# A two-layer cross-attention kernel: the scores of a visit in two PSUM tiles, all maxima at once, and softmax portions recorded ahead of a product

## The chip, the cores and the metric

The kernel runs on one core of a Trainium2 chip. TensorE (PE) multiplies matrices and writes PSUM, VectorE (DVE) and ScalarE (ACT) read PSUM and work on SBUF, GpSimd (POOL) and SyncE (SP) issue DMAs, and POOL adds a few sums. All data are float32. The metric is the device time of one execution in microseconds (us); several executions give a median.

## The reference

Two cross-attention layers follow each other, for 8 batch elements with 100 query tokens of width 640, in 20 heads of 32. The context has 722 tokens of width 1024: 77 text tokens and 645 "ip" tokens. A layer attends to both parts, with a softmax over each part by itself:

```
q  = x @ Wq;  k, v = text @ Wk, text @ Wv;  k_ip, v_ip = ip @ Wk_ip, ip @ Wv_ip      (split into 20 heads)
layer 0:  a = softmax(q k^T * scale) v + softmax(q k_ip^T * scale) v_ip
layer 1:  sem = scale * (softmax(q_full k_full^T * scale) @ text) @ ip^T             (one for all heads)
          a = softmax(q k^T * scale) v + mask * softmax(q k_ip^T * scale + 0.5 * sem) v_ip
x  = a @ Wo + bias + x
```

## The kernel before

A unit `u` is one batch element in one layer: 0 to 7 are layer 0, 8 to 15 layer 1. Units go in pairs. The main loop makes 80 visits `(u, c)`: a visit is the attention of one unit for one group of four heads (`c` from 0 to 4, four heads of 32 in the 128 partitions).

**The attention of a visit.** `scores(u, c, part)` multiplies q and k of four heads: part 0 gives the first 512 ip columns, part 1 the other 133 ip columns and the 77 text columns. Both parts write one PSUM tile `sc` of four banks, a bank for each head. Of each part DVE takes the negative maximum of each row (in layer 0 L953, one instruction for several heads; in layer 1 L960, one for each head, which also adds `sem` and writes the sum to SBUF), and ACT takes the exponential with that maximum as bias and sums it up (L968, one for each head). Text columns have their own maximum, addition and exponential (L974, L976, L984). Small instructions (L979 to L991) turn the two partial maxima and sums into factors; `scaled` (L997, ACT) and `scaled_rest` (L1001, L1005, DVE) multiply the probabilities. In the visit after, `transposes` has TensorE transpose them in six blocks (`pspt`, L1030), which DVE (L1037) or ACT (L1035) copy to SBUF, and `values` multiplies them with v (`pv`) and copies the result out (L1056).

**Portions.** These steps aren't recorded at once. `scores` records the first maxima and puts the rest as portions (closures) into the list `later`. A portion is taken from it by `emit(1)`, which `next_task` calls after each production task that has time of its own; by `free_scores()` at the start of `scores`, as far as the tile `sc` must be free; and by `transposes(..., 0)`, which takes all that are left.

**Production.** The keys and values of the pairs to come are made in between, by Strassen-Winograd products with seven products in place of eight: `seven()` gives seven tasks (L179 to L226), each with products on TensorE and then a copy from PSUM on ACT (first L193, second L202) or an addition on DVE (sixth L198, seventh L208, fifth L213, fourth L219, third L224). The names are psk for keys, psv for values, and psvk for the `two_chunks` products of the last pair. Sums of tokens and of weights that the products need are DVE work (L134 to L137 for the weights, `weight_sums`; L232, L233 and others for the tokens; and, for `two_chunks`, the `begin` task with two later sums, L725 and L726). `spread` gives every task a due time from estimated costs; `make` and `apart` take the tasks due.

**Small work.** `between` splits each visit into four stretches and puts small steps there: `out_piece` (the output product `pso` of a finished pair, and the addition of bias and residual L863), `q_piece` (the queries of layer 1), and in layer 1 the four steps of `sem` (`sem_text` with the copy `g`, `sem_logits`, `sem_transpose` with the copy `tpt`, `sem_scores` with the copy `sem`). They and `pspt` share one PSUM pool.

**The order of the engines.** Only TensorE's is pinned:

```
    with tc.manual_schedule(engines={mybir.EngineType.PE}):
```

Its instructions run as recorded. For DVE, ACT, POOL and SP the framework's scheduler chooses an order from what is recorded; each engine then runs its queue strictly in that order.

Of the kernel before, what the change touches and what calls it, by code (L numbers as in the profile page):

```python
# [9 lines left out]
F32 = mybir.dt.float32  # L10
AF = mybir.ActivationFunctionType
ALU = mybir.AluOpType
AX = mybir.AxisListType

P = 128
B = 8
S = 100
C = 640
CC = 1024
NT = 77  # L20
NI = 645
# [3 lines left out]
KB = NK - KA  # L25
# [19 lines left out]
def two_layer_xattn(  # L45
# [17 lines left out]
    nc = tc.nc  # L63
# [636 lines left out]
    def last_visits(visits):  # L700

        xs, lists = {}, []
        for i, (j, tasks_of) in enumerate(visits):

            def begin(i=i):
                if i == 0:
                    xs.update(places[LAST])
                elif i + 2 < len(visits):
                    xs[i + 2] = load_x(LAST, visits[i + 2][0])

            lists.append([(0.0, begin)] + tasks_of(j, xs, i))
        return lists

    def two_chunks(r, j, xs, at):
        n0, n1 = BLOCKS[j]
        n = n1 - n0
        sums, o, made, late = {}, {}, {}, []

        def begin():
            t = spool.tile([P, 3, HK, 2, NX], F32, tag="s", name=f"sl_{r}_{j}")  # L720
            a11, a12, a21, a22 = quarters(xs[at], n)
            s1, s2, s4 = (t[:, i, :, 0, :n] for i in range(3))
            sums.update(token_sums(a11, a12, a21, a22, s1, s2, None, s4))
            sums[7] = a21
            late.append(lambda: nc.vector.tensor_tensor(a21, a11, a21, ALU.subtract))  # L725
            late.append(lambda: nc.vector.tensor_tensor(s4, a12, s2, ALU.subtract))  # L726
            o[0] = opool.tile([P, 2, 2, P + NX], F32, tag="made", name=f"vko_{r}_{j}")

        def product(ps, which, go_on):
            for k in range(HK):  # L730
                nc.tensor.matmul(
                    ps[:, :P], lhsT=sums[which][:, k, :P], rhs=W["v", WHICH[which]][:, k, r * P : (r + 1) * P],
                    start=(k == 0 and not go_on), stop=(k == HK - 1), skip_group_check=True,
                )
            for k in range(HK):
                nc.tensor.matmul(
                    ps[:, P : P + n], lhsT=W["k", WHICH[which]][:, k, r * P : (r + 1) * P], rhs=sums[which][:, k, :],
                    start=False, stop=(k == HK - 1), skip_group_check=True,
                )

        def step(i):
            if i == 0:
                made[0] = seven(
                    f"psvk_{r}_{j}", product, tuple(o[0][:, h, m, : P + n] for h in range(2) for m in range(2))
                )
            made[0][i]()
            if i < 6:
                return
            for h, u in enumerate(LAST):
                nc.gpsimd.dma_start(  # L750
                    k_d[u][:, :4, n0:n1].rearrange("p (m r) n -> p r m n", r=2)[:, r], o[0][:, h, :, P : P + n]
                )
                nc.gpsimd.dma_start(
                    v_d[u][j * P : (j + 1) * P, : 4 * P].rearrange("p (m r n) -> p r m n", m=2, r=2)[:, r],
                    o[0][:, h, :, :P],
                )

        steps = [(1.8, lambda i=i: step(i)) for i in range(7)]
        sums_ = [(0.0, lambda i=i: late[i]()) for i in range(2)]
        return [(0.0, begin)] + steps[:1] + sums_[:1] + steps[1:4] + sums_[1:] + steps[4:]  # L760

    def fifth_chunk(kinds, j, xs, at):
        n0, n1 = BLOCKS[j]
        tasks = []
        for kind in kinds:
# [28 lines left out]
                        nc.gpsimd.dma_start(v_d[u][j * P : (j + 1) * P, 4 * P :], t[:, i, :P])  # L794

            tasks += [(1.8, lambda h=h, f=half: f(h)) for h in range(2)]
        return tasks


    sem_state, gs = {}, {}  # L800
# [125 lines left out]
    def emit(n):  # L926
        for _ in range(n):
            later.pop(0)[1]()

    def free_scores():  # L930

        emit(max([i + 1 for i, (r, _) in enumerate(later) if r], default=0))

    def scores(u, c, part):
        k0, k1 = ((0, KA), (KA, NK))[part]
        free_scores()
        if part == 0:
            pr[u, c] = ppool.tile([S, 4, NK], F32, tag="p", name=f"p_{u}_{c}")

            stats[u, c] = stat.tile([S, 14, 4], F32, tag="st", name=f"st_{u}_{c}")  # L940
        sc = ps_sc.tile([P, 4, 512], F32, tag="sc", name=f"sc_{u}_{c}_{part}")
        for i in range(4):
            rows = slice(32 * i, 32 * i + 32)
            nc.tensor.matmul(  # L944
                sc[:S, i, : k1 - k0], lhsT=qs_[u][rows, c, :], rhs=ks[u, c][rows, k0:k1], start=True, stop=True
            )
        p, st, l = pr[u, c], stats[u, c], u // B
        n = min(k1, NI) - k0
        lo, f, rz, mul = st[:, 6, :], st[:, 7:9, :], st[:, 9:11, :], st[:, 11:13, :]

        def maxima(heads):
            if l == 0:
                nc.vector.tensor_reduce(  # L953
                    st[:, part, heads[0] : heads[-1] + 1], sc[:S, heads[0] : heads[-1] + 1, :n], AX.X, ALU.max,
                    negate=True,
                )
                return
            for i in heads:

                nc.vector.tensor_tensor_reduce(  # L960
                    out=p[:, i, k0 : k0 + n], in0=sc[:S, i, :n], in1=sems[u][:, k0 : k0 + n], scale=-1.0,
                    scalar=3.0e38, op0=ALU.add, op1=ALU.min, accum_out=st[:, part, i : i + 1],
                )

        def exponentials(heads):
            for i in heads:
                dst = p[:, i, k0 : k0 + n]
                nc.scalar.activation(  # L968
                    dst, dst if l else sc[:S, i, :n], AF.Exp, bias=st[:, part, i : i + 1],
                    scale=-1.0 if l else 1.0, accum_out=st[:, 3 + part, i : i + 1],  # L970
                )

        def text_maxima():
            nc.vector.tensor_reduce(st[:, 2, :], sc[:S, :, n:KB], AX.X, ALU.max, negate=True)  # L974

            nc.vector.tensor_tensor(  # L976
                p[:, :, NI:], sc[:S, :, n:KB], st[:, 2, :].unsqueeze(2).to_broadcast([S, 4, NT]), ALU.add
            )
            nc.vector.tensor_tensor(lo, st[:, 0, :], st[:, 1, :], ALU.min)  # L979
            nc.vector.tensor_tensor(f, lo.unsqueeze(1).to_broadcast([S, 2, 4]), st[:, 0:2, :], ALU.subtract)  # L980

        def text_exponentials():
            nc.scalar.activation(f, f, AF.Exp)
            nc.scalar.activation(p[:, :, NI:], p[:, :, NI:], AF.Exp)  # L984
            nc.vector.tensor_reduce(st[:, 5, :], p[:, :, NI:], AX.X, ALU.add)
            nc.vector.tensor_tensor(st[:, 3:5, :], st[:, 3:5, :], f, ALU.mult)
            nc.vector.tensor_tensor(st[:, 4, :], st[:, 3, :], st[:, 4, :], ALU.add)

        def factors():
            nc.vector.reciprocal(rz, st[:, 4:6, :])  # L990
            nc.vector.scalar_tensor_tensor(  # L991
                mul, f, mask_sb[:, l : l + 1], rz[:, 0:1, :].to_broadcast([S, 2, 4]), ALU.mult, ALU.mult
            )

        def scaled(heads):
            for i in heads:
                nc.scalar.activation(p[:, i, :KA], p[:, i, :KA], AF.Copy, scale=mul[:, 0, i : i + 1])  # L997

        def scaled_rest(text):
# [4 lines left out]
            else:  # L1004
# [2 lines left out]
                    ALU.mult,  # L1007
                )

        if part == 0:  # L1010
            maxima((0, 1))
            later.append((True, lambda: (exponentials((0, 1)), maxima((2, 3)))))
            later.append((True, lambda: exponentials((2, 3))))
        else:
            maxima((0, 1, 2, 3))
            later.append((True, lambda: (exponentials((0, 1, 2, 3)), text_maxima())))
            later.append((False, text_exponentials))
            later.append((False, lambda: (factors(), scaled((0, 1)), scaled_rest(False))))
            later.append((False, lambda: (scaled((2, 3)), scaled_rest(True))))

    pts = {}

# [38 lines left out]
    def production():  # L1061
# [44 lines left out]
        for kinds, js in (("kv", every[:2]), ("k", every[2:]), ("v", every[2:])):  # L1106
            visits += [(j, lambda j, xs, i, kinds=kinds: fifth_chunk(kinds, j, xs, i)) for j in js]
        lists = last_visits(visits)
        lists[0][1:1] = v_last[2:3]
        lists[0][3:3] = v_last[3:]  # L1110
        for a, b, tasks in (
            (n - 10 - AHEAD, n + 2.9, lists[: 2 * NB]),
            (n + 2.9, n + 6.9, lists[2 * NB : 3 * NB]),
# [97 lines left out]
    with tc.manual_schedule(engines={mybir.EngineType.PE}):  # L1211
# [6 lines left out]
        done = [0]  # L1218

        def next_task():  # L1220
            todo[done[0]][2]()
            if todo[done[0]][0] and later:
                emit(1)
            done[0] += 1

        def make(until):
# [13 lines left out]
        def between(n, a, b, small):  # L1240

            mark[0] = done[0]
            near = 0.4 if n < NC_ * LAST[0] + 6 else 0.1
            for i, (_, f) in enumerate(small):
                make(n + a + (b - a) * (i + 1) / (len(small) + 1))
                apart(n + b + near)
                f()
            make(n + b)
            apart(n + b + near)
# [86 lines left out]
```

## Time and profile before

| | |
|---|---|
| Median of 3 runs (lowest to highest) | 2071.68 us (2071.6 to 2073.09) |
| Profiled execution | 2071.6 us |
| Its span, between first and last instruction | 2069.8 us |
| Mean granted TensorE clock | 0.998 of full speed |
| PE busy | 2043.5 us (99%) |
| PE's weight loads busy (beside its products) | 1581.2 us (76%) |
| DVE busy | 1074.8 us (52%) |
| ACT busy | 799.6 us (39%) |
| POOL busy | 309.9 us (15%) |

A line of the timeline gives start and duration in us, engine, source line, operation, what it writes and from what, and how many instructions are taken together; in brackets stand the engine's idle time before it and the instruction that ended it ("1.51 <-ACT p L968": idle for 1.51 us until ACT's line 968, which wrote p, was done). A duration holds the instruction's own latency, so that the start of the next can lie before its end. A line of the waits names the waiting engine and line, what it waited for, the time in total, how often, and the longest.

### The profile page before, as it was taken

The numbers are of one execution on the slowest core, as the hardware profiler recorded it, in microseconds if no ns is written. First come the engines' busy times: TensorE is split into PE (matmuls) and PEld (weight loads), VectorE is DVE, ScalarE is ACT, GpSimd is POOL, SyncE is SP. The second block draws the span as 40 slices with busy tenths as digits, with TensorE's granted clock in tenths as the row PEclk, the third lists the DMA queues.
The fourth block names the chain that finished last, engine by engine and source line by source line (L and its number), as shares of the span: only waits on it lengthen the run. The fifth ranks groups of instructions, "written<-read, shape, count | busy, mean of one in ns | idle before, by whom it ended". The sixth has DMA issues, their size and how long they took to land.

```text
span 2069.8 us, 38196 instructions
## 1 busy us (share of the span) xinstructions
PE 2043.5 (99%) x15122; PEld 1581.2 (76%) x15122; DVE 1074.8 (52%) x2789; ACT 799.6 (39%) x2271; POOL 309.9 (15%) x445
## 2 busy tenths in 40 slices
PE   9999999999999999999989999999999999999998
PEld 8676767677778777786778777787778778889787
DVE  2211322355554655455475555455555557777676
ACT  1001000244433434344333444435444445565576
POOL 3212312111111111010110111010111111111120
PEclk9999999999999999999999999999999999999999
DMA  9545313232424433262543533262434345545472
GB/s 327 155 132 171 97 56 105 88 107 71 129 83 131 129 113 91 81 179 65 160 133 103 147 105 106 72 178 75 115 89 134 90 133 151 158 133 140 121 211 74
DMA packets 302544, 255.35 MB, mean 123 GB/s; under 512 B 46686, under 2 KB 271378, under 8 KB 302366
## 3 DMA queue, kind: packets, MB, share of 16 engines
q1 hardware_dynamic: 280590, 184.48, 32.2%
q0 software_dynamic: 21776, 68.44, 9.5%
q8 instruction: 119, 1.95, 0.4%
q14 instruction: 59, 0.48, 0.1%
HBM read 183.93 MB, written 68.93 MB: 122 GB/s over the span
## 4 chain that ended last, share of the span: by engine, by line
PE 95%; DVE 2%; DMA 1%; ACT 1%; issue 1%; POOL 0%; SPq 0%; ACTq 0%; DVEq 0%
PE psv_a L597 8%; PE psv_d L597 8%; PE pspt L1030 8%; PE psk_d L625 6%; PE psk_a L625 6%; PE sc L944 6%; PE psk L563 5%; PE psv_e L597 4%; PE pv L1052 4%; PE psv_c L597 4%; PE psv_b L597 4%; PE psk_e L625 3%; PE psk_c L625 3%; PE psk_b L625 3%; PE pso L858 3%; PE psq L275 2%
## 5 line engine op out<-in xcount | busy, mean ns | idle before, releaser
L968 ACT ACTIVATE p<-sc,st 100x512 f32<-100x512 f32 (+1 forms) x320 | 166.4, 528 | 218.5 <-DVE st L953 218.2
L1037 DVE COPY pt<-pspt 128x400 f32<-128x400 f32 x319 | 175.5, 569 | 122.8 <-PE pspt L1030 116.6
L997 ACT ACTIVATE p<-p,st 100x512 f32<-100x512 f32 x320 | 208.5, 713 | 62.8 <-DVE st L991 62.7
L968 ACT ACTIVATE p<-p,st 100x512 f32<-100x512 f32 (+1 forms) x320 | 177.1, 555 | 132.3 <-DVE st L960 131.8
L1030 PEld LDWEIGHTS pspt<-ident,p 100*128 100x128 f32 (+1 forms) x1920 | 188.0, 137 | 42.1 <-issue 5.0
L1030 PE MATMUL pspt<-ident,p 100*128 100x100 f32 (+1 forms) x1920 | 211.0, 250 | 5.7 <-DVE res L863 2.4
L597 PE MATMUL psv_a<-wv,x 128*128 128x397 f32 (+1 forms) x560 | 185.0, 472 | 1.3 <-ACT vo L193 1.3
L646 POOL DMA_DIRECT2D k_d<-ko x140 | 99.5, 715 | 527.6 <-DVE ko L219 470.9
L597 PE MATMUL psv_d<-wv,s 128*128 128x320 f32 (+1 forms) x560 | 174.9, 455 | 0.0
L1035 ACT COPY pt<-pspt 128x400 f32<-128x400 f32 (+1 forms) x161 | 78.4, 487 | 227.7 <-PE pspt L1030 227.3
L953 DVE TENSOR_REDUCE st<-sc 100x2 f32<-100x1024 f32 (+1 forms) x120 | 126.3, 1052 | 59.4 <-ACT p L968 30.5
L597 PEld LDWEIGHTS psv_a<-wv,x 128*128 128x128 f32 x560 | 103.5, 190 | 63.7 <-issue 8.1
L960 DVE CUSTOM_DVE_ANT_0 p<-sc,sem 100x512 f32<-100x512 f32 (+1 forms) x320 | 139.7, 489 | 22.5 <-PE sc L944 22.3
L597 PEld LDWEIGHTS psv_d<-wv,s 128*128 128x128 f32 x560 | 103.4, 190 | 57.4 <-issue 5.5
L625 PE MATMUL psk_a<-x,wk 128*128 128x256 f32 (+1 forms) x672 | 137.2, 350 | 4.2 <-ACT ko L193 4.2
L944 PE MATMUL sc<-k,q 32*100 32x210 f32 (+1 forms) x1280 | 138.6, 502 | 0.8 <-ACT p L968 0.6
L625 PE MATMUL psk_d<-s,wk 128*128 128x256 f32 (+1 forms) x672 | 136.4, 348 | 0.0
L612 POOL DMA_DIRECT2D v_d<-vo x70 | 38.3, 548 | 642.4 <-DVE gst L587 317.5
L563 PE MATMUL psk<-x,wk 128*128 128x256 f32 (+1 forms) x560 | 132.0, 383 | 0.0
L625 PEld LDWEIGHTS psk_a<-x,wk 128*128 128x128 f32 x672 | 110.8, 192 | 24.7 <-issue 6.0
L563 PEld LDWEIGHTS psk<-x,wk 128*128 128x128 f32 x560 | 102.8, 189 | 25.7 <-issue 9.9
L625 PEld LDWEIGHTS psk_d<-s,wk 128*128 128x128 f32 x672 | 108.3, 189 | 17.5 <-issue 5.2
(209 smaller groups left out, 3234.5 us busy)
## 6 DMA issues: line engine op xcount, KB each, us to landing
x<-ip_t SPq DMA_DIRECT2D x84, 512.0 KB
k<-k_d SPq DMA_DIRECT2D x80, 322.5 KB
v<-v_d SPq DMA_DIRECT2D x80, 320.0 KB
v_d<-vo POOLq DMA_DIRECT2D x70, 320.0 KB, 2.5
k_d<-ko POOLq DMA_DIRECT2D x112, 128.0 KB, 4.3
x<-ip_t SPq DMA_DIRECT2D x22, 532.0 KB
o<-wo SPq DMA_DIRECT2D x35, 320.0 KB
q<-wq SPq DMA_DIRECT2D x20, 320.0 KB
```

The source lines that it names most:

```text
L563: nc.tensor.matmul(ps[:, : 2 * n], lhsT=W["k", 4][:, k, :], rhs=x_all[:, at[j], :, k, :n], start=(k == 0), stop=(k == NCC - 1),)
L597: nc.tensor.matmul(ps[:, :m], lhsT=tokens(k)[:, :P], rhs=w[:, k, :], start=(k == 0 and not go_on), stop=(k == HK - 1), skip_group_check=True,)
L625: nc.tensor.matmul(ps[:, i * m : (i + 1) * m], lhsT=W["k", WHICH[which]][:, k, r * P : (r + 1) * P], rhs=tokens(k), start=(i == 0 and k == ...
L646: nc.gpsimd.dma_start(dst[:, :, r], ko[0][:, h, :, i, p0 : p0 + n])
L944: nc.tensor.matmul(sc[:S, i, : k1 - k0], lhsT=qs_[u][rows, c, :], rhs=ks[u, c][rows, k0:k1], start=True, stop=True)
L953: nc.vector.tensor_reduce(st[:, part, heads[0] : heads[-1] + 1], sc[:S, heads[0] : heads[-1] + 1, :n], AX.X, ALU.max, negate=True,)
L960: nc.vector.tensor_tensor_reduce(out=p[:, i, k0 : k0 + n], in0=sc[:S, i, :n], in1=sems[u][:, k0 : k0 + n], scale=-1.0, scalar=3.0e38, op0= ...
L968: nc.scalar.activation(dst, dst if l else sc[:S, i, :n], AF.Exp, bias=st[:, part, i : i + 1], scale=-1.0 if l else 1.0, accum_out=st[:, 3 ...
L997: nc.scalar.activation(p[:, i, :KA], p[:, i, :KA], AF.Copy, scale=mul[:, 0, i : i + 1])
L1030: nc.tensor.transpose(ps[:rows, i * S : (i + 1) * S], pr[u, c][:, i, j * P : j * P + rows], ident[:S, :S])
L1037: nc.vector.tensor_copy(dst, src)
L1052: nc.tensor.matmul(ps[32 * i : 32 * i + 32, :S], lhsT=lhs, rhs=pt[:rows, j, i * S : (i + 1) * S], start=(j == 0), stop=(j == 5),)
```

## The change

1. `scores` writes two tiles `sc0` and `sc1` of two banks (heads 0 and 1, heads 2 and 3) in place of one of four.
2. The maxima of all four heads are recorded at once, by pairs of heads. In layer 0, part 1, these are two instructions in place of one; the text maxima and the text addition also go by halves, and are recorded with them, the differences too. The later portions are shared out anew: `factors` and the 133 columns of `scaled_rest` in one, the scaling by ACT in the two after it.
3. Part 0 first takes all that is left in `later`; part 1 calls `free_scores()` as before.
4. `next_task` takes a portion before the task in place of after it, and `between` takes one before each small step.
5. The token sums of a visit of the last pair's products (`begin` of `two_chunks`) are joined to the last task of the visit before; two parts of the last weight sums move to later places in the first list.

```diff
--- before.py
+++ after.py
@@ -708,7 +708,12 @@
                 elif i + 2 < len(visits):
                     xs[i + 2] = load_x(LAST, visits[i + 2][0])
 
-            lists.append([(0.0, begin)] + tasks_of(j, xs, i))
+            first_sums, tasks = tasks_of(j, xs, i)
+            if first_sums and i:
+
+                t, f = lists[-1][-1]
+                lists[-1][-1] = (t, lambda f=f, g=first_sums: (f(), g()))
+            lists.append([(0.0, begin)] + ([(0.0, first_sums)] if first_sums and not i else []) + tasks)
         return lists
 
     def two_chunks(r, j, xs, at):
@@ -757,7 +762,7 @@
 
         steps = [(1.8, lambda i=i: step(i)) for i in range(7)]
         sums_ = [(0.0, lambda i=i: late[i]()) for i in range(2)]
-        return [(0.0, begin)] + steps[:1] + sums_[:1] + steps[1:4] + sums_[1:] + steps[4:]
+        return begin, steps[:1] + sums_[:1] + steps[1:4] + sums_[1:] + steps[4:]
 
     def fifth_chunk(kinds, j, xs, at):
         n0, n1 = BLOCKS[j]
@@ -794,7 +799,7 @@
                         nc.gpsimd.dma_start(v_d[u][j * P : (j + 1) * P, 4 * P :], t[:, i, :P])
 
             tasks += [(1.8, lambda h=h, f=half: f(h)) for h in range(2)]
-        return tasks
+        return None, tasks
 
 
     sem_state, gs = {}, {}
@@ -933,60 +938,65 @@
 
     def scores(u, c, part):
         k0, k1 = ((0, KA), (KA, NK))[part]
-        free_scores()
         if part == 0:
+            emit(len(later))
             pr[u, c] = ppool.tile([S, 4, NK], F32, tag="p", name=f"p_{u}_{c}")
 
             stats[u, c] = stat.tile([S, 14, 4], F32, tag="st", name=f"st_{u}_{c}")
-        sc = ps_sc.tile([P, 4, 512], F32, tag="sc", name=f"sc_{u}_{c}_{part}")
+        else:
+            free_scores()
+
+        scs = [ps_sc.tile([P, 2, 512], F32, tag=f"sc{h}", name=f"sc_{u}_{c}_{part}_{h}") for h in range(2)]
         for i in range(4):
             rows = slice(32 * i, 32 * i + 32)
             nc.tensor.matmul(
-                sc[:S, i, : k1 - k0], lhsT=qs_[u][rows, c, :], rhs=ks[u, c][rows, k0:k1], start=True, stop=True
+                scs[i // 2][:S, i % 2, : k1 - k0], lhsT=qs_[u][rows, c, :], rhs=ks[u, c][rows, k0:k1], start=True, stop=True
             )
         p, st, l = pr[u, c], stats[u, c], u // B
         n = min(k1, NI) - k0
         lo, f, rz, mul = st[:, 6, :], st[:, 7:9, :], st[:, 9:11, :], st[:, 11:13, :]
 
-        def maxima(heads):
+        def maxima(h):
             if l == 0:
                 nc.vector.tensor_reduce(
-                    st[:, part, heads[0] : heads[-1] + 1], sc[:S, heads[0] : heads[-1] + 1, :n], AX.X, ALU.max,
-                    negate=True,
+                    st[:, part, 2 * h : 2 * h + 2], scs[h][:S, :, :n], AX.X, ALU.max, negate=True
                 )
                 return
-            for i in heads:
+            for i in (2 * h, 2 * h + 1):
 
                 nc.vector.tensor_tensor_reduce(
-                    out=p[:, i, k0 : k0 + n], in0=sc[:S, i, :n], in1=sems[u][:, k0 : k0 + n], scale=-1.0,
+                    out=p[:, i, k0 : k0 + n], in0=scs[h][:S, i % 2, :n], in1=sems[u][:, k0 : k0 + n], scale=-1.0,
                     scalar=3.0e38, op0=ALU.add, op1=ALU.min, accum_out=st[:, part, i : i + 1],
                 )
 
-        def exponentials(heads):
-            for i in heads:
+        def exponentials(h):
+            for i in (2 * h, 2 * h + 1):
                 dst = p[:, i, k0 : k0 + n]
                 nc.scalar.activation(
-                    dst, dst if l else sc[:S, i, :n], AF.Exp, bias=st[:, part, i : i + 1],
+                    dst, dst if l else scs[h][:S, i % 2, :n], AF.Exp, bias=st[:, part, i : i + 1],
                     scale=-1.0 if l else 1.0, accum_out=st[:, 3 + part, i : i + 1],
                 )
 
-        def text_maxima():
-            nc.vector.tensor_reduce(st[:, 2, :], sc[:S, :, n:KB], AX.X, ALU.max, negate=True)
-
+        def text_maxima(h):
+            heads = slice(2 * h, 2 * h + 2)
+            nc.vector.tensor_reduce(st[:, 2, heads], scs[h][:S, :, n:KB], AX.X, ALU.max, negate=True)
             nc.vector.tensor_tensor(
-                p[:, :, NI:], sc[:S, :, n:KB], st[:, 2, :].unsqueeze(2).to_broadcast([S, 4, NT]), ALU.add
+                p[:, heads, NI:], scs[h][:S, :, n:KB], st[:, 2, heads].unsqueeze(2).to_broadcast([S, 2, NT]), ALU.add
             )
+
+        def differences():
+
             nc.vector.tensor_tensor(lo, st[:, 0, :], st[:, 1, :], ALU.min)
             nc.vector.tensor_tensor(f, lo.unsqueeze(1).to_broadcast([S, 2, 4]), st[:, 0:2, :], ALU.subtract)
 
         def text_exponentials():
             nc.scalar.activation(f, f, AF.Exp)
             nc.scalar.activation(p[:, :, NI:], p[:, :, NI:], AF.Exp)
+
+        def factors():
             nc.vector.tensor_reduce(st[:, 5, :], p[:, :, NI:], AX.X, ALU.add)
             nc.vector.tensor_tensor(st[:, 3:5, :], st[:, 3:5, :], f, ALU.mult)
             nc.vector.tensor_tensor(st[:, 4, :], st[:, 3, :], st[:, 4, :], ALU.add)
-
-        def factors():
             nc.vector.reciprocal(rz, st[:, 4:6, :])
             nc.vector.scalar_tensor_tensor(
                 mul, f, mask_sb[:, l : l + 1], rz[:, 0:1, :].to_broadcast([S, 2, 4]), ALU.mult, ALU.mult
@@ -1007,16 +1017,19 @@
                     ALU.mult,
                 )
 
+        for h in range(2):
+            maxima(h)
         if part == 0:
-            maxima((0, 1))
-            later.append((True, lambda: (exponentials((0, 1)), maxima((2, 3)))))
-            later.append((True, lambda: exponentials((2, 3))))
+            later.append((True, lambda: exponentials(0)))
+            later.append((True, lambda: exponentials(1)))
         else:
-            maxima((0, 1, 2, 3))
-            later.append((True, lambda: (exponentials((0, 1, 2, 3)), text_maxima())))
-            later.append((False, text_exponentials))
-            later.append((False, lambda: (factors(), scaled((0, 1)), scaled_rest(False))))
-            later.append((False, lambda: (scaled((2, 3)), scaled_rest(True))))
+            for h in range(2):
+                text_maxima(h)
+            differences()
+            later.append((True, lambda: (exponentials(0), exponentials(1), text_exponentials())))
+            later.append((False, lambda: (factors(), scaled_rest(False))))
+            later.append((False, lambda: (scaled((0, 1)), scaled_rest(True))))
+            later.append((False, lambda: scaled((2, 3))))
 
     pts = {}
 
@@ -1106,8 +1119,9 @@
         for kinds, js in (("kv", every[:2]), ("k", every[2:]), ("v", every[2:])):
             visits += [(j, lambda j, xs, i, kinds=kinds: fifth_chunk(kinds, j, xs, i)) for j in js]
         lists = last_visits(visits)
-        lists[0][1:1] = v_last[2:3]
-        lists[0][3:3] = v_last[3:]
+
+        lists[0][5:5] = v_last[2:3]
+        lists[0][7:7] = v_last[3:]
         for a, b, tasks in (
             (n - 10 - AHEAD, n + 2.9, lists[: 2 * NB]),
             (n + 2.9, n + 6.9, lists[2 * NB : 3 * NB]),
@@ -1218,9 +1232,10 @@
         done = [0]
 
         def next_task():
-            todo[done[0]][2]()
+
             if todo[done[0]][0] and later:
                 emit(1)
+            todo[done[0]][2]()
             done[0] += 1
 
         def make(until):
@@ -1244,6 +1259,8 @@
             for i, (_, f) in enumerate(small):
                 make(n + a + (b - a) * (i + 1) / (len(small) + 1))
                 apart(n + b + near)
+                if later:
+                    emit(1)
                 f()
             make(n + b)
             apart(n + b + near)
```

TensorE's order stays the same, but that the four score products of a part go to two tiles. SP's and POOL's orders stay the same, but for one exchange of two neighbouring loads of k at the end. DVE and ACT have other orders. Where a first copy L193 stood behind one or two of a visit's exponentials over 512 columns, it now stands behind two or four (layer 0 shows both); the addition L863 of some `out_piece` steps now stands behind the factors and both parts of `scaled_rest`.

## Prediction

> **What bounds the kernel now.** I read the page's first part, then the chain that ended last, then the waits of TensorE alone, then the timeline around each wait. TensorE is busy for 2043.5 us of a span of 2069.8 us (99%), DVE for 52%, ACT for 39%. The profiled execution took 2071.6 us, 1.8 us of it outside the span, and the median of the three runs is 2071.68 us. A measurement here tells about 0.2% (4.1 us) from no change.
>
> ```profile
> PE 95%; DVE 2%; DMA 1%; ACT 1%; issue 1%; POOL 0%; SPq 0%; ACTq 0%; DVEq 0%
> ```
>
> The chain is TensorE almost throughout, so work taken from or given to DVE and ACT counts only where TensorE then waits more or less. TensorE's waits by releaser, with total, number and longest:
>
> ```profile
> PE psk_a L625 <- ACT ko L193: 4.2, 1, 4.2
> PE pspt L1030 <- DVE res L863: 2.4, 11, 0.6
> PE psk_c L625 <- DVE ko L198: 1.5, 1, 1.5
> PE pskt_d L316 <- issue: 1.4, 1, 1.4
> PE psv_a L597 <- ACT vo L193: 1.3, 1, 1.3
> ```
>
> Nearly all are product copies (ACT L193), product additions (DVE L198) or the residual addition (DVE L863). The scores' own wait, sc behind the exponentials L968, is 0.6 us plus ticks, so there is hardly anything to win at the scores. What matters is how near the other rows stand to their product. Around 1356 us, DVE alone:
>
> ```profile
> 1355.91 0.20 DVE L990 RECIPROCAL st<-st 100x8 f32<-100x8 f32 x1
> 1356.33 0.42 DVE L863 SCALAR_TENSOR_TENSOR res<-pso,bias_sb,res 128x200 f32<-128x200 f32 x1 [0.22 <-PE pso L858]
> 1356.68 0.57 DVE L1037 COPY pt<-pspt 128x400 f32<-128x400 f32 x1
> 1357.17 0.22 DVE L991 SCALAR_TENSOR_TENSOR st<-st,mask_sb 100x8 f32<-100x8 f32 x1
> 1357.30 0.47 DVE L1001 TENSOR_TENSOR p<-p,st 100x308 f32<-100x308 f32 x1
> 1357.69 0.70 DVE L1005 TENSOR_TENSOR p<-p,st 100x532 f32<-100x532 f32 x1
> ```
>
> L863 frees a buffer for the last transposes (pspt), which start at 1356.81, 0.06 us after L863's end: no slack, any delay is TensorE's. And around 458 us:
>
> ```profile
> 457.46 0.68 ACT L968 ACTIVATE p<-sc,st 100x512 f32<-100x512 f32 x1
> 458.03 0.20 ACT L968 ACTIVATION_READ_ACCUMULATOR p<-sc,st 100x1 f32 x1
> 458.12 0.42 ACT L193 COPY vo<-psv_a 128x320 f32<-128x320 f32 x1
> 458.26 1.23 DVE L953 TENSOR_REDUCE st<-sc 100x2 f32<-100x1024 f32 x1 [1.51 <-ACT p L968]
> ```
>
> The copy L193 stands behind two exponentials and ends at 458.54; TensorE goes on with psv_a at 458.89, a slack of 0.35 us.
>
> **The change, part by part.** TensorE's order is unchanged; the score products only go to other tiles, four heads at a time as before: 0. SP's and POOL's orders are unchanged but for a swap of two loads at the end, so no transfer is moved past another queue: 0. The added DVE instructions (the 711-ns maxima over 532 columns in layer 0, the 474-ns text maxima and 476-ns text addition, each cut in two): each cut costs about 0.12 us of DVE, the fixed part of these rows ((711-474)/(532-308) = 1.06 ns an element leaves 474-308*1.06 = 148 ns, some of it overlapped by the next). That is three cuts in each of 40 visits and two in the other 40, 200*0.12 = 24 us, hidden behind TensorE with DVE at 52%; in the last layer, at 72 to 77%, it would cost by the waits counted below.
>
> *Gains.* Part 1 of the scores no longer waits for a late exponential: 0.6 us at 1167 and two ticks of 0.17: **-1.0**. One long wait changes shape, at 1037 us:
>
> ```profile
> 1037.67 1.49 DVE L134 TENSOR_TENSOR wvt<-wv,wv 128x1280 f32<-128x1280 f32 x1 [4.98 <-DMA wv<-wvi]
> 1039.08 1.22 DVE L953 TENSOR_REDUCE st<-sc 100x2 f32<-100x1024 f32 x1
> ...
> 1041.01 0.37 ACT L193 COPY ko<-psk_a 128x266 f32<-128x266 f32 x1
> ...
> 1041.43 3.62 PE L625 MATMUL psk_a<-x,wk 128*128 128x133 f32 x16 [4.19 <-ACT ko L193]
> ```
>
> The weight sum L134 waits for its load; maxima, exponential and copy stand behind it. In the changed order the first maxima stand ahead of L134, so the copy is early and psk_a runs from 1037.2 to 1039.2. Then psk_c must wait for the addition L198, which still stands behind L134, L135, L136 and one maxima and ends at 1043.44. psk_c started at 1045.58, so up to 2.1 us are won. But a wait of 3.6 us (1039.9, after eight transposes, to 1043.5) stays. Behind the 4.19-us wait the sixteen matmuls took 3.62 us instead of the 1.98 of psk_b before it, with a granted clock of 0.78 from 1042 to 1048; behind the 1.54-us wait at 1726 they took 2.09. 3.6 is nearer to 4.19, so I charge the slow product again: 2.1-1.6 = **-0.5** (bounds -0.5 and -2.1). [...] At 1066 us TensorE would start psv_a earlier, but psv_c there waits for L198, with the same DVE work ahead of it in both orders: 0.
>
> *Losses.* (a) A portion is now asked for before the small work and before the product, so L991, L1001 and L1005, and what leads to them, stand ahead of L863. In layer 1 (1357, 1790, 1958 us) the chain before them ended at 1356.11; L991's 0.13 and 0.39 and 0.63 us to the next starts make 1.15, so L863 would start at 1357.35 instead of 1356.33: +1.0 each. In layer 0 (653, 888, 1128 us) the text exponentials come earlier in the changed order, so between 0 and 1.4 us each; middle 0.7. 3*1.0+3*0.7 = **+5.1** (0 to 7.5).
>
> (b) All maxima run at once, so all four exponentials can stand ahead of the first copy. Where they do, L193 moves by two exponentials, 2*0.68 = 1.36 us. At 459 and 1294 us, slack 0.35 and 0.32: **+2.0**. At 437 and 523 us (slack 1.13) and 567 and 802 us (1.23): 2*0.23+2*0.13 = **+0.7**. Elsewhere the slack is larger. Together 0 to 4.
>
> (c) In layer 1 the same move of 1.36 us meets the copies that feed transposes (g, tpt, sem) and the two-chunk products of the last pair. The slacks are 0.05 us at 1815, 0.61 at 1863, 0.55 at 1895, 0.56 at 1914; at 1937, with a slack of 0.05, one exponential (0.71) is added: 1.3+0.75+0.8+0.8+0.66 = **+4.3** (0 to 6).
>
> (d) At 1726 us the addition L198 goes behind the fourth maxima (0.61 us) with no slack, unless DVE came to it earlier: 0 to +0.6; about ten places in which slack and move agree within 0.3 us: 0 to +2. I take 0 for both, as their cover (idle DVE and ACT) is visible.
>
> Sum: -1.5+5.1+2.0+0.7+4.3 = +10.6, and 2071.6+10.6 is about **2082 us**. Losing all bounds gives 2071.6-1.5+7.5+4+6+2.6 = 2090; losing none 2071.6-3.1 = 2068.5.
>
> **Rivals.** *Faster (0.18):* the portions asked for earlier pull the whole softmax chain ahead, so that what stalls today vanishes: 1.0 and 2.1 as above, the 2.4 us of L863, and the waits of pv and pspt for ACT's pt copies (0.9 each): 7.3 us, **2064.3 us**. It decides at the end of pso: DVE would have to finish L1005 by 1356.3, and its chain (L985 at 1355.13) would have to start 1.2 us earlier. Against it: that chain hangs on the text exponentials, which end at 1355.10 behind the four 133-wide ones in both orders. For it: layer 0, where the text maxima came late.
> *No change (0.15):* DVE and ACT are idle half the time, the moved rows slide into that, and gains and a part of the losses cancel: **2071.6 us**, within 4. Against it are slacks of 0.05 us.
> *Much slower (0.03):* two tiles break the concurrency of the four heads. Their two groups start 0.51 us apart in part 0 (1.04 us in all) and take 0.54 us in part 1; run one after the other, they would add about 1.0 and 0.5 us in each of 80 visits, 120 us, **2190 us**. No wait stands between the tiles' matmuls, so it is unlikely.
> The forecast as summed has 0.64. Its own range is 2076 to 2090.
>
> **How the numbers follow.** Slower is 0.64+0.03 = 0.67, faster 0.18, same 0.15. For 8 in 10, the range takes the forecast's own, no change and half of the faster case: 2066 to 2092.
>
> **What would show it.** The waits of pspt for DVE res should grow from 2.4 us in 11 to some 7, with the lines that answer to L991, L1001 and L1005 ahead of the addition in the timeline; psv_a should wait for L193 near 459 and 1294 us; g and tpt waits should appear from 1815 us on; psk_a's 4.2 us should be gone and a wait of psk_c for L198 be there. TensorE's busy time should stay within 2 us, DVE's grow by about 24. If the sc groups take longer, or res waits stay at 2.4 us, I am wrong.

## The result and the profile after

The changed kernel takes 2080.21 us (median of 6 runs, 2079.47 to 2082.53) against 2070.93 us of the kernel before, run beside it (6 runs, 2068.57 to 2073.09): a ratio of 1.0047, 95% interval 1.0034 to 1.006. It is slower by some 9 us; the prediction said 2082. The profiled execution took 2081.3 us with a span of 2079.5 us, 9.7 us more than before, at the same mean clock of 0.998.

TensorE's waits in the profile after, by releaser, with total, number and longest. Source lines moved down by five to thirteen: L868 is the residual addition (L863 before), L1043 the transposes, L838 and L825 the copies g and tpt.

```profile
PE pspt L1043 <- DVE res L868: 6.9, 11, 1.2
PE psq L275 <- DMA wq<-wq: 4.8, 1, 4.8
PE psk_c L625 <- DVE ko L198: 4.6, 2, 2.3
PE pspt L1043 <- ACT g L838: 2.2, 3, 1.1
PE pskt_d L316 <- issue: 1.8, 1, 1.8
PE pspt L1043 <- ACT tpt L825: 1.4, 2, 0.7
PE psv_a L597 <- ACT vo L193: 1.4, 3, 0.6
```

The waits for res grew from 2.4 to 6.9 us, those for g from 0.2 to 2.2 us, tpt appears, and psk_a's 4.2 us is gone while psk_c, with one wait of 1.5 us before, waits twice, for 4.6 us together. The residual addition at 1357 us, DVE alone:

```profile
1355.88 0.23 DVE L1001 SCALAR_TENSOR_TENSOR st<-st,mask_sb 100x8 f32<-100x8 f32 x1
1356.02 0.47 DVE L1011 TENSOR_TENSOR p<-p,st 100x308 f32<-100x308 f32 x1
1356.41 0.70 DVE L1015 TENSOR_TENSOR p<-p,st 100x532 f32<-100x532 f32 x1
1357.04 0.42 DVE L868 SCALAR_TENSOR_TENSOR res<-pso,bias_sb,res 128x200 f32<-128x200 f32 x1
```

Before, the three rows stood behind the addition; now the addition follows them without a gap. And ACT at 459 us, where the copy now stands behind four exponentials (the last two are shown):

```profile
458.30 0.69 ACT L975 ACTIVATE p<-sc,st 100x512 f32<-100x512 f32 x1
458.87 0.21 ACT L975 ACTIVATION_READ_ACCUMULATOR p<-sc,st 100x1 f32 x1
458.96 0.69 ACT L975 ACTIVATE p<-sc,st 100x512 f32<-100x512 f32 x1
459.54 0.21 ACT L975 ACTIVATION_READ_ACCUMULATOR p<-sc,st 100x1 f32 x1
459.63 0.44 ACT L193 COPY vo<-psv_a 128x320 f32<-128x320 f32 x1
```

TensorE's order is the same in both kernels, so each of its products can be set against itself, and the difference of the two starts, here called the shift, steps up where time is lost and down where it is won. It begins at 0.31 us and ends at 9.70 us:

| Where | Shift, us | Prediction |
|---|---|---|
| residual additions: 653, 888, 1128 us: 0.59, 0.59, 0.58; 1357, 1790, 1958 us: 1.06, 1.00, 0.99 | +4.8 | +5.1 (a) |
| copies L193 in layer 0: 437 and 523 us 0.34 each, 459 us 0.83, 1294 us 0.62, 567 and 802 us 0.17 each, 1090 us 0.21 | +2.7 | +2.7 (b) |
| copies in layer 1: 1815 us 1.28, 1863 us 0.63, 1895 us 0.98, 1914 us 0.96, 1937 us 0.71 | +4.6 | +4.3 (c) |
| psk_c at 1726 us: 0.73 longer wait, 1.65 slow clock | +2.4 | 0 (d) |
| weight sums: 1037 us -3.4, 1066 us -0.5 | -3.9 | -0.5 |
| scores: 1167 us -0.7; 693 and 929 us -0.17 each | -1.0 | -1.0 |
| smaller steps | -0.2 | 0 |

At the weight sums, the profile after shows (DVE alone):

```profile
1039.11 1.49 DVE L134 TENSOR_TENSOR wvt<-wv,wv 128x1280 f32<-128x1280 f32 x1 [1.60 <-DMA wv<-wvi]
1040.52 1.22 DVE L961 TENSOR_REDUCE st<-sc 100x2 f32<-100x1024 f32 x1
1041.66 1.48 DVE L135 TENSOR_TENSOR wvt<-wvt,wv 128x1280 f32<-128x1280 f32 x1
1043.06 1.48 DVE L136 TENSOR_TENSOR wv<-wv,wv 128x1280 f32<-128x1280 f32 x1
1044.46 0.43 DVE L198 TENSOR_TENSOR ko<-psk_b,ko 128x266 f32<-128x266 f32 x1
```

TensorE's products there, and the psk_c at 1728 us:

```profile
1039.93 1.99 PE L625 MATMUL psk_a<-x,wk 128*128 128x133 f32 x16
1041.76 0.85 PE L1043 MATMUL pspt<-ident,p 100*128 100x100 f32 x8
1044.94 2.09 PE L625 MATMUL psk_c<-x,wkt 128*128 128x133 f32 x16 [2.33 <-DVE ko L198]
...
1728.47 2.90 PE L625 MATMUL psk_c<-x,wkt 128*128 128x133 f32 x16 [2.27 <-DVE ko L198]
```

psk_a ran from 1039.93, without a wait, and psk_c waited from the transposes' end for L198, 2.33 us, until 1044.94. The clock tells why this place gained more than forecast and the one at 1728 us lost more. In the records of all profiles here the granted clock changes only at steps of 3.41 us. Five of these stretches of the profile after; the columns are busy time and instructions of PE, PEld, DVE, ACT and POOL, then the granted clock, the DMA share and GB/s:

```profile
1040.08:1043.49 3.41, 2.53 (x25) 2.34 (x23) 3.41 (x4) 1.45 (x4) 0.00 (x0) 1.00 0.60 179
1043.49:1046.91 3.42, 1.97 (x17) 1.97 (x18) 3.42 (x5) 0.38 (x1) 0.00 (x0) 1.00 1.00 295
1046.91:1050.32 3.41, 3.41 (x36) 3.01 (x35) 1.86 (x5) 0.49 (x1) 0.00 (x0) 1.00 0.07 8
...
1726.17:1729.58 3.41, 1.15 (x10) 1.11 (x10) 3.38 (x7) 2.64 (x8) 0.00 (x0) 1.00 0.58 154
1729.58:1732.99 3.41, 3.41 (x19) 3.41 (x18) 1.25 (x3) 0.00 (x0) 0.00 (x0) 0.50 0.00 0
```

The wait of 2.33 us is divided between two stretches, with 0.88 and 1.44 us of idle time, and the clock stayed at 1.00. The wait of 2.27 us at 1728 us lies in one stretch, and in the next the clock was 0.50.

### The profile page after: what moved, and what is told of

The parts are those of the page before. It is cut to its first block, busy times and chain, and to the rows that moved or that the text cites. A ratio compares the mean times of both kernels' runs of the same rounds, so it can differ in the third digit from the quotient of the medians.

```text
span 2079.5 us, 38497 instructions
## 1 busy us (share of the span) xinstructions
PE 2045.9 (98%) x15122; PEld 1581.5 (76%) x15122; DVE 1077.5 (52%) x2989; ACT 790.7 (38%) x2271; POOL 309.5 (15%) x445
## 5 line engine op out<-in xcount | busy, mean ns | idle before, releaser
L1043 PEld LDWEIGHTS pspt<-ident,p 100*128 100x128 f32 (+1 forms) x1920 | 188.6, 138 | 50.8 <-DVE res L868 8.9
L1043 PE MATMUL pspt<-ident,p 100*128 100x100 f32 (+1 forms) x1920 | 212.5, 251 | 13.4 <-DVE res L868 6.9
L952 PE MATMUL sc<-k,q 32*100 32x210 f32 (+1 forms) x1280 | 138.5, 502 | 0.0
```

Of the source, the lines that this page charges most:

```text
L952: nc.tensor.matmul(scs[i // 2][:S, i % 2, : k1 - k0], lhsT=qs_[u][rows, c, :], rhs=ks[u, c][rows, k0:k1], start=True, stop=True)
L1043: nc.tensor.transpose(ps[:rows, i * S : (i + 1) * S], pr[u, c][:, i, j * P : j * P + rows], ident[:S, :S])
```

## The experiments

Two theories stood against each other at the start: that the portions asked for earlier push rows ahead of the additions and copies (theory P, the prediction's), or that the two tiles let the scheduler choose another order, and the places of the portions hardly matter (T, later S). TensorE's pinned order is kept in all kernels, so the shift can be read in each. The times of before, beside them, were 2071.7, 2069.84, 2071.64 and 2071.23 us in the four groups of runs.

**The portions alone.** One tile; only these edits:

```diff
         def next_task():
-            todo[done[0]][2]()
             if todo[done[0]][0] and later:
                 emit(1)
+            todo[done[0]][2]()
...
                 apart(n + b + near)
+                if later:
+                    emit(1)
                 f()
```

> The kernel before with only the two new places at which a portion is asked for (ahead of a task in next_task, ahead of each small step in between); one score tile, old portions. Theory P (the portions asked for earlier put rows ahead of the residual addition, the copies and the additions): pspt waits for res rise from 2.4 us to 6 or 7, and the copies L193 move; about 2078 us. Rival T (the two tiles, with all maxima free to run at once, let the scheduler change the order, the places of the portions hardly matter): res waits stay near 2.4 us, 2069 to 2073 us.

Measured: 2076.49 us, ratio 1.0024 (1.0015 to 1.0033). In its waits the residual additions are as before:

```profile
PE psk_a L625 <- ACT ko L193: 3.5, 1, 3.5
PE psk_c L625 <- DVE ko L198: 2.4, 1, 2.4
PE pspt L1030 <- DVE res L863: 2.4, 11, 0.6
PE psv_a L597 <- ACT vo L193: 2.3, 1, 2.3
```

Up to 1000 us its shift doesn't move at all (0.24 us at 450 and at 1000 us). The loss sits at the two weight-sum places (+1.7 us at 1041 to 1069 us, +2.7 at 1726, slow products in both) and one tpt copy (1.0). Theory P fails as the cause of the res and L193 delays; the time was between the two forecasts, so the portions by themselves do cost time, but at other places.

**The two tiles alone.** Old portions; the maxima of heads 2 and 3 still asked for behind the first exponentials:

```diff
-        sc = ps_sc.tile([P, 4, 512], F32, tag="sc", name=f"sc_{u}_{c}_{part}")
+        scs = [ps_sc.tile([P, 2, 512], F32, tag=f"sc{h}", name=f"sc_{u}_{c}_{part}_{h}") for h in range(2)]
...
-                sc[:S, i, : k1 - k0], lhsT=qs_[u][rows, c, :], rhs=ks[u, c][rows, k0:k1], start=True, stop=True
+                scs[i // 2][:S, i % 2, : k1 - k0], lhsT=qs_[u][rows, c, :], rhs=ks[u, c][rows, k0:k1], start=True, stop=True
```

> The kernel before with the scores in two tiles of two banks, and the text maxima and addition by halves, which that needs; portions and their places as before. Theory P: the gains alone, the 4.2 us wait of psk_a gone, res waits about 2.4 us, 2067 us. Rival T: most of the changed kernel's loss, with the copies L193 behind four exponentials, g and tpt waits from 1815 us on, a longer wait of psk_c at 1726 us; res waits about 5 us; 2077 to 2080 us.

Measured: 2081.79 us, ratio 1.0052 (1.0037 to 1.0067): the whole loss, by this part alone. Parts 3 and 5 of the change weren't run by themselves; the loss comes without them.

```profile
PE pspt L1032 <- DVE res L863: 6.5, 11, 1.2
PE psk_c L625 <- DVE ko L198: 4.8, 2, 2.6
PE psq L275 <- DMA wq<-wq: 4.5, 1, 4.5
PE psv_a L597 <- ACT vo L193: 3.2, 3, 2.0
PE pspt L1032 <- ACT g L833: 2.2, 3, 1.1
```

But for psv_a's longest, 2.0 us in place of 0.6, these are the changed kernel's waits, nearly number by number. Theory T holds for the additions and copies: with two tiles the scheduler puts both maxima, then all four exponentials, ahead of the copy, and the factors ahead of the residual addition, wherever the portions are recorded. Why it chooses so isn't shown; nor were the halved text rows, which two tiles need, tried in one tile.

**All maxima at once, in one tile.**

```diff
             maxima((0, 1))
-            later.append((True, lambda: (exponentials((0, 1)), maxima((2, 3)))))
+            maxima((2, 3))
+            later.append((True, lambda: exponentials((0, 1))))
```

> The kernel before with the maxima of heads 2 and 3 of part 0 recorded at once, in the old one tile of four banks; the portions as before but for that. Theory S (it is the two tiles that let the scheduler put all four exponentials ahead of the copies and the factors ahead of the residual addition): res waits stay at 2.4 us, no g or tpt waits are added, 2068 to 2074 us. Rival (recording the maxima at once is enough): the changed kernel's waits, 2077 us or more.

Measured: 2069.82 us, ratio 0.9992 (0.9983 to 1.0001), no difference; res waits 2.4 us, no g or tpt waits. For (a), (b) and (c) the maxima at once aren't the cause, the split tile is. For the weight sums they do by themselves what the whole change does: psk_a's wait goes, psk_c waits twice (6.0 us together, the longest 3.7) with half-rate products behind both waits, and at 1726 us the shift rises by 2.5 us, so loss (d) needs no second tile. The score wait at 1167 us is won here too (-0.68 us). Of this profile's shift, which ends at -0.4 us, 1.6 us are chance: near 1939 us the profile before has a half-rate stretch and this one hasn't.

**Without the portion ahead of small steps**: the changed kernel without `if later: emit(1)` in `between`.

> The changed kernel without the portion that between asks for ahead of each small step. Theory P: the waits of pspt for res fall from 6.9 us back to about 2.4, and 2080.2 becomes about 2075.5 us. Rival T: only the last row of scaled_rest (0.63 us) leaves the way of the residual addition, and only in the three pieces of layer 1: res waits about 5 us, about 2078.3 us.

Measured: 2080.68 us, ratio 1.0041 (1.0028 to 1.0055). The res waits fell from 6.9 to 5.6 us: 0.62 us each at 1357 and 1790 us, which is L1015's step to the next row, and nothing at the other four. So this portion has a small share of (a), and by the waits the expectation of theory T was the nearer; the time, expected at 2078.3 us, didn't tell.

**The portion after the task again**: `next_task` as before, the rest as changed.

> The changed kernel with next_task taking its portion after the task again, as before. Theory S (the scheduler's order hardly depends on these places): within 1.5 us of the changed kernel, with the same waits for res, g, tpt and L193. Rival P (the places ahead of the product cause b and c): 2075 us or less.

Measured: 2080.71 us in 2 runs (ratio 1.0054, 1.0036 to 1.0072). Set against the changed kernel, TensorE's shift steps by more than 0.25 us behind the first 100 us only where a slow product lies at 1047 us in place of 1730, and near 1950 us, by 0.29 us up and then as much down. Asking ahead of a product's additions, by itself, does nothing that this profile shows once the tiles are split. The slow product's place is chance: both kernels wait more than 2 us at both places, and here 1.96 of the 2.50 us at 1043 us fell into one stretch of the clock, and 1.43 of the 2.16 us at 1728 us.

**Pinning ACT too, and then ACT and DVE**: the changed kernel with

```diff
-    with tc.manual_schedule(engines={mybir.EngineType.PE}):
+    with tc.manual_schedule(engines={mybir.EngineType.PE, mybir.EngineType.Activation}):
```

> The changed kernel with ACT's order pinned as recorded too (TensorE and ACT; DVE, POOL and SP chosen by the scheduler). In the recorded order the copies L193 and g stand behind two of a visit's first exponentials again, tpt still behind four. Theory S (the two tiles let the scheduler put all four exponentials ahead of the copies, and that is loss b and part of c): the delays at 437, 459, 523 and 1294 us (2.1 us in all) and the 1.3 us at 1815 us go, 2076 to 2077 us. Rival (the portions asked for ahead of a product cause these delays, in whichever order): they stay, 2080 us.

Measured: 2080.0 us (4 runs, ratio 1.0054, 1.0038 to 1.0069). In the profile the copies stand behind two exponentials again, as at 457 us:

```profile
456.73 0.68 ACT L975 ACTIVATE p<-sc,st 100x512 f32<-100x512 f32 x1
457.30 0.20 ACT L975 ACTIVATION_READ_ACCUMULATOR p<-sc,st 100x1 f32 x1
457.39 0.42 ACT L193 COPY vo<-psv_a 128x320 f32<-128x320 f32 x1
```

Against the changed kernel the shift loses 0.34, 0.83, 0.34 us at 437, 459 and 523 us, 0.62 at 1294 and 0.63 at 1863 us: loss (b) is the scheduler's order of ACT. At 1815 us nothing moved: the copy g still stood behind four exponentials, which the expectation had misread. With 0.17 each at 567 and 802 us that is 3.1 of the 3.6 us by which the shift ends lower. The gain shows in the profile; the four timed runs, 2077.96 to 2081.81 us, don't confirm it. That stays open.

> The changed kernel with ACT's and DVE's order pinned as recorded too. The weight sums L134 to L137 no longer stand ahead of the addition L198 that psk_c waits for, at 1044 and 1728 us; the residual addition still has a row of scaled_rest ahead of it. Theory S: the two psk_c waits (4.6 us, and the slow clock behind one, 1.5 us), and the losses b and part of c go; res waits stay near 5 us: 2068 to 2071 us, not above before. Rival (DVE then waits at the head of its queue for things that the scheduler had moved away, tokens or weights that have not come): new waits of TensorE for DVE, 2080 us or more.

Measured: 2089.16 us, ratio 1.0095 (1.0081 to 1.0109). The rival was right. Set against the kernel before, the weight-sum place at 1037 us gained 6.0 us, but res waits grew to 10.8 us and new ones came (7.3 us for the exponential tp, 2.5 us for token sums): the recorded order holds more back than it frees.

**Two tiles in units 5 and 6 alone**, by closing the pool and opening it with other tiles at the two borders:

```diff
+        if split != sc_pool[1]:
+            sc_stack.close()
+            sc_pool[:] = [sc_stack.enter_context(tc.tile_pool(name=f"ps_sc{int(split)}_{name}", bufs=1, space=PSUM)), split]
```

> The kernel before with two score tiles in the visits of units 5 and 6 alone (other visits keep one tile of four banks; the pool is closed and opened again at the two borders). Both theories: the weight-sum places at 1037 and 1066 us gain about 4 us and the score wait at 1167 us 0.7, with little lost in these units, so 2066 to 2067 us against 2070.9 of before. Against it: closing the pool holds up TensorE at a border by some us, or the clock falls behind the wait of psk_c that stays, then 2068 to 2072 us.

Measured: 2072.72 us, ratio 1.0005 (0.9996 to 1.0014): no gain. psk_a's wait and its slow product went, but psk_c then waited 2.5 us for L198 with a slow product behind it, psv_a at 1066 us waited 2.0 us, and the addition at 1128 us cost 0.87. So the changed kernel's -3.9 us at the weight sums isn't the split's to keep: there TensorE came 2.85 us late to it, and its wait was divided between two stretches of the clock, while the 2.5 us here were followed by a half-rate one.

**The weight sums off DVE.** The kernel before, with the v sums of the two later loads on POOL:

```diff
-    def weight_sums(kind, n, engines=None):
+    def weight_sums(kind, n, engines=None, all_on=None):
...
-        first, then = engines or (nc.vector, nc.vector)
+        first, then = engines or (all_on or nc.vector, all_on or nc.vector)
...
-                parts[kind] = weight_sums(kind, n)
+                parts[kind] = weight_sums(kind, n, all_on=nc.gpsimd if kind in 'v' else None)
```

> The kernel before with the v weight sums of the two later loads (eight instructions, L134 to L137) on POOL in place of DVE; nothing else. Theory (the places at 1037 and 1726 us are DVE held by L134, which waits for its load, with maxima and the addition L198 behind it): the waits of psk_a (4.2 us) and psk_c (1.5 us) and the slow products behind the first (1.6 us) go, 2071 becomes about 2064 us. Rival (POOL's sums take 3.3 us each and come too late for the v products, or hold up its stores): a new wait of psv, 2070 us or more.

Measured: 2063.55 us, ratio 0.9972 (0.9962 to 0.9983), faster than both kernels. POOL alone:

```profile
1034.28 2.67 POOL L134 TENSOR_TENSOR wvt<-wv,wv 128x1280 f32<-128x1280 f32 x1 [4.41 <-DMA wv<-wvi]
1037.03 2.67 POOL L135 TENSOR_TENSOR wvt<-wvt,wv 128x1280 f32<-128x1280 f32 x1
```

L134 now waits for its load on an engine that nothing urgent stands behind. The shift falls by 6.0 us at 1041 us and by 1.8 at 1726; it gives back 2.5 at 1059 us, where psv_a waits 2.27 us behind the k sums on DVE, with a slow product. (Another 2.5 us of this profile's shift come in the first 100 us, ahead of anything changed, and are scatter. Without them the profile ends 4.0 us lower, while the ratio says 5.8; the difference isn't placed.)

**The k sums too** (`'vk'`).

> The kernel before with both the v and the k weight sums of the later loads on POOL. Theory: with the k sums off DVE, the wait of psv_a for L193 near 1059 us (2.3 us, and slow products behind it 1.5 us) goes as well: about 2060 us. Rival (four k sums of some 2.5 us on POOL come late for the k products, or hold up its stores): a new wait, 2063 us or more.

Measured: 2068.67 us, ratio 0.9994 (0.9984 to 1.0004): the gain is gone. DVE in this profile, at 1056 us:

```profile
1055.77 0.69 DVE L232 TENSOR_TENSOR s<-x 128x512 f32<-128x512 f32 x1
1056.49 2.72 DVE L233 TENSOR_TENSOR s<-s,x 128x512 f32<-128x512 f32 x1
1059.13 0.25 DVE L1056 COPY hs<-pv 128x100 f32<-128x100 f32 x1
1059.31 2.66 DVE L543 TENSOR_TENSOR s<-x,s 128x512 f32<-128x512 f32 x1
```

L233 took 2.72 us in place of 0.69, beside POOL's L134 (1053.99 to 1058.66, 4.67 us, where the sums of this size at 1062.49 and 1064.79 took 2.35), and L543 2.66 us, beside POOL's L135 (1058.74 to 1061.41). Maxima, exponentials and copy came late behind them, and psv_a waited 4.66 us. The rival was right on the time; its two reasons weren't seen; what the profile shows is these longer rows on both engines at once.

**The change with the v sums on POOL.**

> The changed kernel with the v weight sums on POOL. Theory: both waits of psk_c for L198 (4.6 us together, and about 1.6 us of slow products behind one) go, the other losses stay: about 2074 us, some 10 us above the kernel before with the same sums on POOL. Rival (the two tiles win as much as they lose once the weight sums no longer stand in the way): 2066 us or less.

Measured: 2075.97 us, ratio 1.002 (1.0011 to 1.0028). Both psk_c waits are gone (-2.4 us from 1000 to 1050 us and -4.2 us from 1700 to 1750 us against the changed kernel, the second with its slow product), and the res, g and tpt waits stand as in the changed kernel (6.8, 2.5 and 1.4 us); psv_a at 1064 us waits 1.0 us longer. By the two ratios, 1.0020/0.9972 = 1.0048, it is some 10 us above the kernel before with the same sums: that is what the change costs where the v sums aren't in the way of either.

**Sums on POOL and all maxima at once in one tile.**

> The kernel before with the v weight sums on POOL and the maxima of heads 2 and 3 of part 0 recorded at once in the one tile. Theory: the 6 to 7 us of the sums, and the 0.7 us of the score wait at 1167 us on top; res waits 2.4 us: 2062 to 2063 us, not to be told from the sums alone. Rival (the copies L193 move behind more exponentials and new waits eat the gain): 2066 us or more.

Measured: 2064.71 us (9 runs), ratio 0.9974 (0.9964 to 0.9984); the score wait is gone, but the total can't be told from the sums alone.

## Why the prediction was right, and where not

*The total, 2082 for 2080.2.* Right, but two wrong terms of it cancel in part: the weight sums at 1037 and 1066 us gained 3.4 us more than taken, 1726 us lost 2.4 us more. Both hold one stretch of half clock, some 1.6 us, that was charged at the first place and came at the second; in no_small_emit and portion_after_task, with waits of like length at both (2.70 and 2.18, 2.50 and 2.16 us), it comes at the first. Which place pays is luck; the two together, -1.5 us for -0.5, can be held against the forecast.

*(a) 5.1 us, measured 4.8.* Right in place, row by row (1.0 each in layer 1; 0.7 taken and 0.59 measured in layer 0) and in mechanism on DVE. Its own steps, 1356.11 and 1.15 us, give a start at 1357.26 and not 1357.35, +0.9 for the +1.0 taken. In layer 0, 0.7 was the middle of a range and no more. Wrong in cause: "a portion is now asked for before the small work" explains 1.2 us of it (no_small_emit). With two tiles alone the rest is there, and with the portions alone none.

*(b) 2.7 us and (c) 4.3, measured 2.7 and 4.6.* Slack against length of the rows moved gave each place to within some 0.2 us, but for 1294 us (1.0 taken, 0.62 measured), which 0.21 at 1090 us, not foreseen, makes up in part. That maxima run at once was named as the reason; the run in one tile shows that it takes the split tile.

*(d) taken as 0, measured 2.4.* The failing step is "their cover (idle DVE and ACT) is visible": psk_c at 1726 us had no slack, so the fourth maxima's 0.61 us had to be charged (0.73 measured), and the slow product behind a wait grown to 2.27 us was not thought of. It comes with the maxima at once, in one tile too.

*The gain of 0.5 at 1037 us, measured 3.4.* The step that failed is the slow product, charged because 3.6 us is near 4.19. The wait came out at 2.33 us, since TensorE came 2.85 us late there (the losses until then) and the load 1.44 us late, and, divided between two stretches, it had no slow product behind it. At 1066 us, -0.5 for 0. The scores, -1.0 as taken.

*The rivals.* Faster did not come: the text exponentials kept their place. Four heads ran concurrently as before (the first and the last of four products start within 0.02 us in both), the scores' rows took 138.5 us for 138.6. DVE's instructions were cut as foreseen, but its busy time grew by 2.7 us and not by 24: the cut rows' own durations grew by 29.6 us (text maxima 37.9 to 49.4, addition 38.1 to 50.2, part 1 maxima 28.4 to 34.4 us), and the rows overlap each other more. TensorE's busy time grew by 2.4 us, a little past the 2 us named as a sign.

## What to carry to other kernels

Where a scheduler orders the engines, splitting a buffer is an edit of the order: compare the orders, list for each wait of the bounding engine its slack and the rows that now stand ahead, and charge the difference place by place. A slack of 0.05 us is a cost of the whole move. And look at what an engine that runs its queue in order is held up by before giving it more to do early (in the profile before, DVE stood idle for 4.98 us at L134, until 1037.67 us, though the maxima behind it had had their scores since 1033.4): here, taking the sums that wait for a load out of the softmax's way won 5.8 us by the ratio, more than half of what the two tiles cost.

## What the runs showed of the hardware

*The clock behind a wait.* In the fourteen profiles the granted clock is 1.00 or 0.50 and changes only at steps of 3.41 us. At 0.50 the products of 16 start every 0.22 us in place of 0.11, and a stretch of it costs some 1.6 us (before, psk_a at 1041.43 us: 3.62 us in place of psk_b's 1.98). Count TensorE's idle time in each stretch between 100 and 2050 us: all 20 stretches with 1.71 us or more were followed by one at 0.50 (among them 3.41 us from 1037.8 us before, 2.27 us from 1726.2 us after), and none of the 14 with 1.37 to 1.67 us (1.54 us from 1723.9 us before, 1.44 us from 1043.5 us after). Ahead of 100 us the profile after has one with 1.75 us, from 60.5 us, that was not. So in the profile after the wait of 2.27 us, in one stretch, cost 1.65 us more, and the wait of 2.33 us, divided into 0.88 and 1.44 us, did not; two or three such places make 3.2 to 4.8 us, about the scatter of the times (4.5 us between the lowest and the highest of the six runs before, 3.1 after). All four waits of 3.5 us or more behind 400 us cost it (4.19 us before, 3.5 in emits_alone, 3.7 in maxima_at_once_one_tile, 4.66 in vk_sums_on_pool). One place is an exception: between 1930 and 1948 us eight profiles have a half-rate stretch behind 0.95 to 1.32 us of idle time (1.00 before, 1.32 after), and five have none behind 0.95 to 1.02; what decides there isn't shown. (Three more such stretches follow a half-rate one.)

*POOL and DVE.* While POOL added two SBUF tensors, a DVE addition of two SBUF tensors beside it took up to 2.72 us in place of 0.69 (L233 at 1056.49 in vk_sums_on_pool), and one of four elements a row 2.49 us in place of 0.16 (L979 at 1042.75 in v_sums_on_pool), while DVE additions with one input in PSUM kept their 0.42 to 0.44 us (L198 at 1034.98 and L208 at 1038.93 in v_sums_on_pool). Not each one was longer: L527, L543 and L232, from 1054.57 us in vk_sums_on_pool, kept their 0.69 us, beside the POOL sum that itself took 4.67 us. The four-element row ended at 1045.24, within 0.02 us of POOL's L137 beside it (1042.53 to 1045.22).
